# The order of the first loads on SyncE's queue, fixed by hand, in a two-layer decoder on one Trainium2 core

## The chip, the core and the metric

The kernel runs on one core of a Trainium2 chip (trn2). The core has a matrix engine (TensorE, PE in the profile, its weight loads PEld), a vector engine (VectorE, DVE), a scalar engine (ScalarE, ACT), a general engine (GpSimd, POOL) and a synchronisation engine (SyncE, SP) that does nothing here but issue transfers. SP issues its transfers one after the other: a transfer that has to wait holds all those behind it. POOL issues the indirect ones (gathers and scatters). Both kinds are carried by the same 16 DMA engines.

The metric is the device time of one execution in microseconds, as the median of several runs. The kernel before took 3494.49 us (three runs, 3491.88 to 3496.33).

## The reference

Eight sequences of 256 tokens with 512 features go through two layers of three residual steps each. All is float32.

```
x = x + L0_attn(layernorm(x))              # 16 heads, rotary, causal window of 64
x = x + L0_xattn(layernorm(x), ctx, mask)  # cross attention over ctx
x = x + L0_ffn(layernorm(x))               # 64 experts, top 6, capacity 192, and a shared one
x = x + L1_attn(layernorm(x))              # Mamba2 scan, chunks of 64
x = x + L1_xattn(layernorm(x), ctx, ctx)   # attention over features
x = x + L1_ffn(layernorm(x))               # 8 low-rank adapters on one wide network
```

Of `L0_attn` the beginning matters here: `qkv = x @ w_qkv.T`, then the rotary turn of q and k with tables `cos` and `sin`, then masked scores. Of `L0_ffn` it matters that each of the 64 experts has its own `Wg`, `Wu` (512x352 each) and `Wd` (352x512), and computes `(silu(buf @ Wg.T) * (buf @ Wu.T)) @ Wd.T` for its 192 slots.

## The kernel before

The 2048 tokens are 16 tiles `x0` to `x15` of 128 tokens; a batch is two of them. They are loaded once, stay in on-chip memory, each stage adds into them, and the last stage writes them out. The stages follow one another: `l0_attention`, `l0_cross` (which carries the routing and the shared expert in its gaps), `l0_experts`, `l1_mamba` (which begins with gathering the experts' results), `l1_cross`, `l1_ffn`.

**Who sets the order.** The program is written as one sequence. A scheduler then chooses for each engine the order in which its instructions stand, except that instructions given to `pin` (line 95) keep the program's order among themselves. Nearly all matmuls are pinned (`mm`, line 99). Of the transfers on SP some are (the context loads of line 441, the shared expert's of 670 to 684), most are not. Which engine waits for what follows from the tiles that an instruction reads and writes.

**Weights.** All large weights go through one pool of eight buffers of 1 MB (`wpool`, line 74). `weight` (line 88) takes a buffer and issues the load on SP; the load waits until the former user of the buffer is done. Such loads were not pinned.

**The first loads.** `load_constants` (line 102) issues, in this order, the table `c_const` (386 KB), the 16 token tiles (256 KB each), `c_cols`, `c_rows` (1035 KB, one row spread over 128 partitions), `c_small`, and `norm`. Then `l0_attention` (line 182) issues the three projection weights q, k, v (1024 KB each), the output weight `wo`, and the table `const0` with mask, `cos` and `sin` (576 KB). `load_constants` also fills `nhalf`, which `layernorm` reads.

**The start of l0_attention.** For each batch, `normal` normalises the two token tiles on DVE (statistics, then one pass; the root on POOL), `turn` turns them on PE and ACT copies the result to `xnT`, `features` projects 256 features of q or k (called for k0, q0, k1, q1) and turns them by the rotary tables: an ACT copy, a DVE shuffle, two POOL products, a DVE sum. `values` projects v. `step` makes scores and masked maxima. Work of later batches is laid between that of earlier ones (table `between`).

**The expert stage.** `l0_experts` (line 881) handles experts in pairs. Its loads and the products that use them:

```
def load(pair, h):                                     # line 906
    w["g", h] = self.weight(a["Wg"][e]...)             # 704 KB
    w["u", h] = self.weight(a["Wu"][e]...)             # 704 KB
    nc.sync.dma_start(wd[:, 0, :], a["Wd"][e, :P, :])  # 256 KB, line 913
    nc.sync.dma_start(wd[:112, 1:, :], ...)            # 448 KB, line 914
```

`hidden(pair, h, m)` computes one of three blocks of an expert's hidden layer, with eight matmuls on Wg's columns ahead of eight on Wu's (as the trace counts them). `first(pair, h)` multiplies the first 128 slots by Wd, and writes the result to `y_d` on SP (line 939). `last(pair)` does so for the other 64 slots of both experts (two writes, line 954). On PE, a pair p goes in this order:

```
hidden(p,0,0)  first(p-1,1)  last(p-1)  hidden(p,0,1)  hidden(p,0,2)  turn
hidden(p,1,0)  first(p,0)    hidden(p,1,1)  turn  hidden(p,1,2)  turn
```

`turn` transposes gathered tokens `xg` of the next pair, which POOL gathers from `xn_d` (line 893). The writes to `y_d` are not pinned.

Of the kernel before, what the change touches and what calls it, by code (L numbers as in the profile page):

```python
# [7 lines left out]
F32 = mybir.dt.float32  # L8
# [10 lines left out]
P = 128  # L19
B, S, D = 8, 256, 512  # L20
T = B * S
NT = T // P
HC = D // P
# [24 lines left out]
NORM_W = {"sel": 56, "spread": HC * P}  # L48

COL_W = {"bq": 4, "bk": 4, "conv_b": 6, "conv_w": 24, "norm_w": 4, "b1": 16, "end": 1}  # L50

ROW_W = {
    "bv": D, "bo": D, "ln_g": D, "ln_b": D, "br": E1,
    "dt_bias": NH1, "A_log": NH1, "D": NH1, "res": 1, "gamma": 1,
}

SMALL_W = {"gate": HC * E0, "wr": HC * E1, "wdt": HC * NH1}
# [3 lines left out]
def offsets(widths):  # L61
    at, out = 0, {}
    for name, w in widths.items():
        out[name] = (at, at + w)
        at += w
    return out


class Decoder:
# [18 lines left out]
    def weight(self, src, n, w, rows=P):  # L88

        t = self.wpool.tile([P, 2048], F32, tag="w", name="w")  # L90
        v = t[:rows, : n * w].rearrange("p (n w) -> p n w", n=n)
        self.nc.sync.dma_start(v, src)
        return v

    def pin(self, ins):
# [3 lines left out]
    def mm(self, out, lhs, rhs, start=True, stop=True):  # L99
        self.pin(self.nc.tensor.matmul(out, lhs, rhs, start=start, stop=stop))  # L100

    def load_constants(self):
        nc, a = self.nc, self.a
        c = self.cpool.tile([P, sum(CONST_W.values())], F32, name="c_const")
        nc.sync.dma_start(c, a["const"])
        for name, (lo, hi) in offsets(CONST_W).items():
            setattr(self, name, c[:, lo:hi])
        self.x = []
        for i in range(NT):
            t = self.xpool.tile([P, D], F32, name=f"x{i}")  # L110
            nc.sync.dma_start(t, a["x"][i * P : (i + 1) * P, :])
            self.x.append(t)
        c = self.cpool.tile([P, sum(COL_W.values())], F32, name="c_cols")
        nc.sync.dma_start(c, a["cols"])
        self.col = {k: c[:, lo:hi] for k, (lo, hi) in offsets(COL_W).items()}
        c = self.cpool.tile([P, sum(ROW_W.values())], F32, name="c_rows")
        nc.sync.dma_start(c, a["rows"].partition_broadcast(P))
        self.row = {k: c[:, lo:hi] for k, (lo, hi) in offsets(ROW_W).items()}
        c = self.cpool.tile([P, sum(SMALL_W.values())], F32, name="c_small")
        nc.sync.dma_start(c, a["small"])  # L120
        self.small = {k: c[:, lo:hi] for k, (lo, hi) in offsets(SMALL_W).items()}
        self.norm = self.stage_constants(self.cpool, "norm", NORM_W)

        self.in_order = False
        self.nhalf = self.cpool.tile([P, 16], F32, name="c_nhalf")
        nc.vector.memset(self.nhalf, -0.5)

    def stage_constants(self, pool, name, widths):
        c = pool.tile([P, sum(widths.values())], F32, name=name)
        self.nc.sync.dma_start(c, self.a[name])  # L130
        return {k: c[:, lo:hi] for k, (lo, hi) in offsets(widths).items()}

    def rsqrt(self, pool, v, eps, tag):
# [48 lines left out]
    def l0_attention(self):  # L182
# [7 lines left out]
        nc, a = self.nc, self.a  # L190
        LEAD = 10
        W = 3 * P // 2
        wq, wk, wv = (
            self.weight(a["wqkv"][:, i * D : (i + 1) * D].rearrange("(c p) o -> p c o", p=P), HC, D)
            for i in range(3)
        )
        wo = self.weight(a["wout0"].rearrange("(c p) o -> p c o", p=P), HC, D)
        head = lambda j: slice(j * HD, (j + 1) * HD)
        half = lambda h: slice(h * S, (h + 1) * S)
        pairs = [i ^ 1 for i in range(32)]  # L200
        with ExitStack() as ctx:
# [7 lines left out]
            nc.vector.tensor_copy(minus, self.third.unsqueeze(2).to_broadcast([P, HC, P]))  # L209
            at = self.stage_constants(one, "const0", STAGE0_W)  # L210
            mask, keep, cos, sin = (at[k] for k in ("mask", "keep", "cos", "sin"))
            sel, spread = self.norm["sel"], self.norm["spread"]
            made = {b: {} for b in range(B)}

# [175 lines left out]
            for n in range(-16, 8 * B + 18):  # L390
                if n >= -LEAD:
                    step(n)
                for lag, which in ((2, "acc"), (3, "sums")):
                    p = n - lag
# [1116 lines left out]
def decode(tc, a, out):  # L1511
    with ExitStack() as ctx:
        d = Decoder(ctx, tc, a, out)
        d.load_constants()
        with ExitStack() as late:
            d.l0_attention()
            combine = d.l0_moe(late)
            d.l1_mamba(combine)
        d.l1_cross()
        d.l1_ffn()  # L1520
# [96 lines left out]
```

## Time and profile before

| | |
|---|---|
| median of the runs | 3494.49 us |
| the profiled execution, by the clock of the runs | 3501.66 us |
| its span in the profile | 3499.9 us |
| mean granted clock of PE | 0.957 |
| PE busy | 3245.4 us |
| 1185 to 1990 us (experts): PE busy, DMA share, GB/s | 802.4 of 805 us, 0.74, 234 |
| 1990 to 2370 us (mamba): PE busy | 294.7 of 380 us |
| 2370 to 2745 us (l1_cross): PE busy | 359.4 of 375 us |

The profile is that of one execution. "Busy" is time in which an engine had an instruction in work. A row of the timeline gives start and length in us, engine, source line, operation, the tiles written and read, how many like it follow each other, and in brackets how long the engine stood idle before and what ended that. SPq rows are the issue of transfers, not the transfer itself. A row of the windows gives for each stretch the length, the busy time of PE, PEld, DVE, ACT and POOL, and last the granted clock of PE (1.00 is full), the share of the 16 DMA engines' time and GB/s. In the table of transfers the last two numbers are the size of one and the us from issue to landing, where a waiting instruction shows it.

### The profile page before, as it was taken

To read this page: it belongs to the slowest core of one execution; us is meant where nothing else is said; L and a number is where in the kernel's file an instruction comes from. 1 tells how busy PE (TensorE), PEld (TensorE's weight loads), DVE (VectorE), ACT (ScalarE), POOL (GpSimd) and SP (SyncE) were. 2 spreads that over 40 slices of the span, in tenths; PEclk is the share of its full clock that TensorE was granted. 3 is DMA by queue.
4 is the path that set the end of the run, shared out by engine and by line. 5 is a ranking of instruction groups with operands and counts; after the bars stand their busy time and mean duration, and the time that the engine had idled before them with its cause. 6 is when DMAs were issued, how large, how long until landed. Compare 5 with 4: busy or idle time off the path is not lost.

```text
span 3499.9 us, 46993 instructions
## 1 busy us (share of the span) xinstructions
PE 3245.4 (93%) x18803; PEld 2111.6 (60%) x18803; DVE 1551.1 (44%) x3744; ACT 994.2 (28%) x1959; POOL 759.5 (22%) x792
## 2 busy tenths in 40 slices
PE   6999888899989899999999767998999899999999
PEld 4666555555555687877777544663444466666665
DVE  3655588777764100000000178665666333333332
ACT  1222123333332122222222123441555322222221
POOL 2222001222225211111110187332111111111111
PEclk9999989999999999999999869997999899999999
DMA  4000020000000477777777653001000000000000
GB/s 173 1 1 1 7 63 18 11 13 13 26 15 21 135 234 240 236 240 232 240 236 238 224 158 100 1 25 54 28 27 17 34 7 7 5 1 7 6 6 12
DMA packets 106810, 272.56 MB, mean 78 GB/s; under 512 B 15136, under 2 KB 23968, under 8 KB 105696
## 3 DMA queue, kind: packets, MB, share of 16 engines
q1 hardware_dynamic: 88128, 219.16, 19.1%
q0 software_dynamic: 18464, 50.40, 5.2%
q8 instruction: 148, 2.42, 0.3%
q14 instruction: 70, 0.57, 0.1%
HBM read 235.81 MB, written 33.70 MB: 77 GB/s over the span
## 4 chain that ended last, share of the span: by engine, by line
PE 66%; DVE 10%; POOL 6%; issue 3%; DMA 1%; ACT 1%; POOLq 0%; SPq 0%; DVEq 0%; ACTq 0%
PE mm L100 17%; PE sc L100 15%; PE out L100 7%; PE w L100 6%; PE s L100 4%; PE a L100 3%; PE b L100 3%; PE sums L100 2%; PE acc L100 2%; PE st L100 2%; POOL map_d L765 1%; PE pt L903 1%; PE rt L100 1%; DVE acc L1043 1%; POOL ye L648 1%
## 5 line engine op out<-in xcount | busy, mean ns | idle before, releaser
L100 PE MATMUL sc<-xgT,w 128*112 128x192 f32 (+1 forms) x3072 | 529.6, 328 | 0.0
L100 PEld LDWEIGHTS sc<-xgT,w 128*112 128x112 f32 (+1 forms) x3072 | 497.4, 182 | 41.1 <-issue 40.9
L929 DVE TENSOR_TENSOR aT<-act,sc 112x192 f32<-112x192 f32 (+1 forms) x192 | 68.0, 354 | 740.9 <-ACT act L928 740.9
L100 PE MATMUL mm<-xnT,w 128*128 128x256 f32 x1152 | 275.9, 395 | 22.0 <-DMA w<-in_wqkv 15.7
L100 PE MATMUL mm<-w,aT 112*128 112x512 f32 (+3 forms) x768 | 262.7, 596 | 0.0
L100 PEld LDWEIGHTS mm<-xnT,w 128*128 128x128 f32 x1152 | 223.7, 198 | 59.1 <-issue 18.5
L100 PE MATMUL w<-xnT,w 128*128 128x256 f32 x1024 | 243.0, 380 | 0.0
L100 PE MATMUL out<-w,mix 128*128 128x512 f32 x512 | 240.4, 592 | 0.0
L1460 DVE TENSOR_TENSOR h<-base,b 128x512 f32<-128x512 f32 x128 | 88.1, 688 | 327.0 <-PE b L100 327.0
L893 POOL DMA_INDIRECT xg<-xn_d,slots x96 | 90.7, 945 | 641.5 <-PE pt L903 634.1
L100 PEld LDWEIGHTS w<-xnT,w 128*128 128x128 f32 x1024 | 192.3, 191 | 61.2 <-issue 40.4
L1464 POOL TENSOR_TENSOR mix<-h 128x256 f32<-128x256 f32 x128 | 92.8, 725 | 610.8 <-DVE h L1462 547.3
L140 POOL TENSOR_TENSOR lnr<-lne,c_nhalf 128x1 f32<-128x1 f32 x112 | 68.9, 619 | 715.1 <-DVE lne L138 585.4
L1321 DVE TENSOR_REDUCE m<-s 128x1 f32<-128x512 f32 x256 | 164.8, 685 | 102.6 <-PE s L100 84.0
L100 PE MATMUL st<-q,k 32*128 32x256 f32 (+1 forms) x1024 | 196.7, 545 | 9.4 <-ACT e L503 9.3
L1270 ACT ACTIVATE e<-st 128x512 f32<-128x512 f32 x256 | 138.9, 595 | 142.3 <-PE st L100 140.6
L928 ACT ACTIVATE act<-sc 112x192 f32<-112x192 f32 (+1 forms) x192 | 63.4, 330 | 402.2 <-PE sc L100 402.2
L100 PEld LDWEIGHTS out<-w,mix 128*128 128x128 f32 x512 | 97.3, 190 | 122.4 <-issue 120.3
L100 PE MATMUL mm<-mT,w 128*118 128x256 f32 (+1 forms) x768 | 169.7, 379 | 1.1 <-DVE hT L821 1.1
L100 PEld LDWEIGHTS mm<-w,aT 112*128 112x128 f32 (+3 forms) x768 | 95.6, 163 | 122.5 <-issue 122.5
L100 PE MATMUL s<-k,q 32*128 32x512 f32 x512 | 159.5, 697 | 6.7 <-issue 3.5
L100 PEld LDWEIGHTS mm<-mT,w 128*118 128x118 f32 (+1 forms) x768 | 138.9, 181 | 34.3 <-issue 7.2
(333 smaller groups left out, 5287.7 us busy)
## 6 DMA issues: line engine op xcount, KB each, us to landing
w<-in_Wg SPq DMA_DIRECT2D x64, 704.0 KB, 8.1
w<-in_Wu SPq DMA_DIRECT2D x64, 704.0 KB, 4.2
w<-in_Wd SPq DMA_DIRECT2D x64, 448.0 KB, 6.7
w<-in_Wd SPq DMA_DIRECT2D x64, 256.0 KB
y_d<-yo SPq DMA_DIRECT2D x64, 256.0 KB, 4.2
y_d<-yo SPq DMA_DIRECT2D x64, 128.0 KB, 4.1
w<-in_W SPq DMA_DIRECT2D x8, 1024.0 KB, 5.1
x<-in_x SPq DMA_DIRECT2D x16, 256.0 KB, 5.7
```

The costliest lines, as they stand in the source:

```text
L100: self.pin(self.nc.tensor.matmul(out, lhs, rhs, start=start, stop=stop))
L140: ins = nc.gpsimd.tensor_tensor(r, e, self.nhalf[:, :n], ALU.pow)
L648: nc.gpsimd.indirect_dma_start(y, None, y_d, bass.IndirectOffsetOnAxis(ap=read[:, k, i : i + 1], axis=0))
L765: self.pin(nc.gpsimd.indirect_dma_start(maps[k % 2], bass.IndirectOffsetOnAxis(ap=work[b]["write"][:, i, k : k + 1], axis=0), tok[:, 2 * b ...
L893: nc.gpsimd.indirect_dma_start(xg, None, xn_d, bass.IndirectOffsetOnAxis(ap=slots[:, i : i + 1], axis=0))
L903: self.pin(nc.tensor.transpose(t[:, blk], w[n][:, blk], self.ident))
L928: nc.scalar.activation(act[:n_m], ps[:n_m, :CAP], AF.Silu)
L929: nc.vector.tensor_tensor(w["a", h][:n_m, m, :], act[:n_m], ps[:n_m, S : S + CAP], ALU.mult)
L1270: nc.scalar.activation(w["e"][kc][:, j, :], st, AF.Exp, scale=SCALE)
L1321: nc.vector.tensor_reduce(m, sc, AX.X, ALU.max)
L1460: nc.vector.tensor_tensor(both(h), twice(base), both(t), ALU.add)
L1464: nc.gpsimd.tensor_tensor(mix, h[:, :G], h[:, G:], ALU.add)
```

## The change

`weight` and `stage_constants` issue through a new `load`, which pins the transfer. The first loads are split into `load_first` (c_const and the first batch's tokens), `load_tokens` (the tokens of one batch) and `load_last` (c_cols, c_rows, c_small). `l0_attention` loads the weights of k, q and v in this order, then `const0`, then the other tokens, `wo`, `norm` and `load_last`. No arithmetic changes.

```
     def weight(self, src, n, w, rows=P):
...
-        self.nc.sync.dma_start(v, src)
+        self.load(v, src)
...
+    def load(self, dst, src):
+        self.pin(self.nc.sync.dma_start(dst, src))
+
-    def load_constants(self):
+    def load_first(self):
...
         c = self.cpool.tile([P, sum(CONST_W.values())], F32, name="c_const")
-        nc.sync.dma_start(c, a["const"])
+        self.load(c, a["const"])
...
+        self.x = [self.xpool.tile([P, D], F32, name=f"x{i}") for i in range(NT)]
+        self.load_tokens(0)
...
+    def load_tokens(self, b):
+        for i in (2 * b, 2 * b + 1):
+            self.load(self.x[i], self.a["x"][i * P : (i + 1) * P, :])
+
+    def load_last(self):
...
     def stage_constants(self, pool, name, widths):
         c = pool.tile([P, sum(widths.values())], F32, name=name)
-        self.nc.sync.dma_start(c, self.a[name])
+        self.load(c, self.a[name])
...
-        wq, wk, wv = (
+        wk, wq, wv = (
...
-            for i in range(3)
+            for i in (1, 0, 2)
         )
-        wo = self.weight(a["wout0"].rearrange("(c p) o -> p c o", p=P), HC, D)
...
             mask, keep, cos, sin = (at[k] for k in ("mask", "keep", "cos", "sin"))
+            for b in range(1, B):
+                self.load_tokens(b)
+            wo = self.weight(a["wout0"].rearrange("(c p) o -> p c o", p=P), HC, D)
+            self.norm = self.stage_constants(self.cpool, "norm", NORM_W)
+            self.load_last()
...
-        d.load_constants()
+        d.load_first()
```

`weight` is called not only there: `l0_cross` (line 410), `l0_experts` (909, 910), `l1_mamba` (986 to 989) and `l1_ffn` (1346 to 1348) load through it. In the program built from the changed kernel, the order on PE and ACT is the same as before; it differs on SP, and on DVE and POOL among the first instructions.

More of the change, by code (lines that the diff above doesn't have):

```diff
@@ L100, in mm @@
         self.pin(self.nc.tensor.matmul(out, lhs, rhs, start=start, stop=stop))
-    def load_constants(self):
+    def load(self, dst, src):
+        self.pin(self.nc.sync.dma_start(dst, src))
+    def load_first(self):
         nc, a = self.nc, self.a
         c = self.cpool.tile([P, sum(CONST_W.values())], F32, name="c_const")
-        nc.sync.dma_start(c, a["const"])
+        self.load(c, a["const"])
         for name, (lo, hi) in offsets(CONST_W).items():
             setattr(self, name, c[:, lo:hi])
[L108 to L122, printed above, removed]
+        self.x = [self.xpool.tile([P, D], F32, name=f"x{i}") for i in range(NT)]
+        self.load_tokens(0)
         self.in_order = False
@@ L126, in load_constants @@
         nc.vector.memset(self.nhalf, -0.5)
+    def load_tokens(self, b):
+        for i in (2 * b, 2 * b + 1):
+            self.load(self.x[i], self.a["x"][i * P : (i + 1) * P, :])
+    def load_last(self):
+        a = self.a
+        c = self.cpool.tile([P, sum(COL_W.values())], F32, name="c_cols")
+        self.load(c, a["cols"])
+        self.col = {k: c[:, lo:hi] for k, (lo, hi) in offsets(COL_W).items()}
+        c = self.cpool.tile([P, sum(ROW_W.values())], F32, name="c_rows")
+        self.load(c, a["rows"].partition_broadcast(P))
+        self.row = {k: c[:, lo:hi] for k, (lo, hi) in offsets(ROW_W).items()}
+        c = self.cpool.tile([P, sum(SMALL_W.values())], F32, name="c_small")
+        self.load(c, a["small"])
+        self.small = {k: c[:, lo:hi] for k, (lo, hi) in offsets(SMALL_W).items()}
     def stage_constants(self, pool, name, widths):
         c = pool.tile([P, sum(widths.values())], F32, name=name)
-        self.nc.sync.dma_start(c, self.a[name])
+        self.load(c, self.a[name])
         return {k: c[:, lo:hi] for k, (lo, hi) in offsets(widths).items()}
```

## The prediction

> **What bounds the kernel now.** I read the page first, then the timeline of the first 45 us, the waits, and one 25 us period of the expert stage.
>
> ```profile
> span 3499.9 us, 46993 instructions
> PE 3245.4 (93%) x18803; PEld 2111.6 (60%) x18803; DVE 1551.1 (44%) x3744; ACT 994.2 (28%) x1959; POOL 759.5 (22%) x792
> PE 66%; DVE 10%; POOL 6%; issue 3%; DMA 1%; ACT 1%; POOLq 0%; SPq 0%; DVEq 0%; ACTq 0%
> ```
>
> TensorE (PE) is busy for 93% of the span and holds 66% of the chain that ended last. A load costs time only where PE stands still for it. At the start it does:
>
> ```profile
> 11.56 0.59 ACT L233 COPY xnT<-mm 128x512 f32<-128x512 f32 x1 [0.27 <-PE mm L232]
> ...
> 14.42 3.31 SPq L92 DMA_DIRECT2D w<-in_wqkv  x3
> ...
> 27.22 15.85 PE L100 MATMUL mm<-xnT,w 128*128 128x256 f32 x64 [15.69 <-DMA w<-in_wqkv]
> ```
>
> Batch 0's tokens are normalised and turned at 12.15 us. The weights are only issued at 14.42, behind all 16 token tiles and four constant tables, and PE stands for 15.69 us. The expert stage is the opposite: in 1185 to 1990 us PE is busy for 802.4 of 805 us, with DMA at 0.74 of its capacity. There the question is how early a load is issued before its use.
>
> ```profile
> 1367.20 5.46 PE L100 MATMUL sc<-xgT,w 128*112 128x192 f32 x32
> 1367.29 0.33 SPq L92 DMA_DIRECT2D w<-in_Wg  x1
> ...
> 1367.95 1.09 SPq L954 DMA_DIRECT2D y_d<-yo  x2
> ...
> 1369.14 0.56 SPq L92 DMA_DIRECT2D w<-in_Wu  x1
> ...
> 1372.68 0.33 SPq L92 DMA_DIRECT2D w<-in_Wg  x1
> ...
> 1378.92 0.33 SPq L939 DMA_DIRECT2D y_d<-yo  x1
> ...
> 1382.64 0.33 SPq L92 DMA_DIRECT2D w<-in_Wu  x1
> ...
> 1384.18 2.77 PE L100 MATMUL sc<-xgT,w 128*128 128x192 f32 x16
> ```
>
> The Wg and Wu issued at 1367.29 and 1369.14 belong to the pair that starts at 1384.18: about 15 us ahead. The Wg and Wu at 1372.68 and 1382.64 belong to that pair's second expert, which starts 13.7 us into it, at 1397.9: again 15 us or more.
>
> **The change part by part.** There are two parts: the first loads get a new order, and every `weight` load in the kernel becomes pinned. I compared SP's queue in the two built programs.
>
> Start. Ahead of wk there stand only c_const, x0 and x1, 386+512 KB. The new queue is these, wk, wq, wv, const0, then x2 to x15, wo, norm and the rest. With wk that is 1.97 MB. By the DMA rows of 0 to 8.5 us the queue had moved so much by 8.2 us; the old wk landed 2.4 us after its bytes were through by the same count (24.8 against 27.2), so wk lands at about 10.6. On VectorE the statistics of x2 and x3 no longer stand ahead of x0's normalisation: the first turn moves from 9.55 to about 8.6, xnT is done near 11.3, and that, not wk, is last. First projection: 27.2 to 11.5, 15.7 us earlier. Price: the statistics of x2 to x8 (7 x 0.69) and three normalisations (3 x 0.55) fall among the rotations of batch 0, 6.5 us of VectorE work that lay in its idle time before. In the new VectorE order x4's statistics and a normalisation precede q0's shuffle, and two normalisations k1's; counted through, the first masked maximum comes some 2.5 us later against PE than before, and PE's second score block waits for it. wq and wv land about 3 and 6 us after wk and are wanted 5.5 us and 16 us after; const0, near 17, is wanted at 18; x2 and x3 likewise. Net -13 us. norm, wo and the tables move behind 8 MB and land by 30 us, before their first use at about 75: nothing.
>
> Expert stage. The pin moves Wg and Wu past the result writes `y_d`, which are not pinned. Built order around one pair, the kernel before above, the changed one below (g2 = Wg of the next pair's first expert, g3 of its second; y0, y1, yy the writes of `first(p,0)`, `first(p,1)`, `last(p)`):
>
> ```
> before: y1(p-1) g2 yy(p-1) u2 d2 d2 g3 y0(p) u3 d3 d3 y1(p) ...
> after:  y0(p) g2 u2 d2 d2 | y1(p) yy(p) g3 u3 d3 d3 | y0(p+1) ...
> ```
>
> So g2, u2 now wait for the result of `first(p,0)`. In the row, that product ends on PE at F = 1378.1, the write is issued at F+0.8, g2 at F+1.25. PE then has 6.1 us of other work until it wants g2 (1384.18), and 7.4 until it wants u2, the second half of that block. Before the change the loads stood 11 us before F, and the Wu at 1382.64 was hidden by a whole 12 us. When does u2 land now? No row shows this burst. Bytes flow about 1 us after issue and at 340 GB/s (270 to 431 in the rows of 1368 to 1373). The write, g2 and u2 are 262+721+721 KB: 5.0 us from F+1.8. Then a tail from last byte to landing, between two rows:
>
> ```profile
> w<-in_Wg SPq DMA_DIRECT2D x1, 704.0 KB, 4.0
> ```
> ```profile
> w<-in_Wd SPq DMA_DIRECT2D x1, 448.0 KB, 5.6
> ```
>
> The first (issued at 1106.9 into an empty queue) gives 4.0-1.0-2.1 = 0.9 us. The second (1358.96, right behind a Wu of 704 KB and with another Wd after it) lands at 1364.6, while 1180 KB from 1358.7 are through at 1362.2: 2.4. u2 has two Wd behind it, so I take 2.1, near the second: F+8.9, a stall of 1.5 us (0.3 to 1.8). For g3, u3: they now follow `last(p)`, which ends at L = 1367.27 in the row; its two writes are issued by L+1.77 and g3 at L+1.87. PE's other work is 5.66 us, 6.95 until u3. g3's bytes flow from L+2.9; 1442 KB take 4.25; with the tail L+9.25: stall 2.3 (1.1 to 2.6). Sum 3.8 us for each of 31 pairs (the first pair's loads don't wait for a write): **+118 us**.
>
> Two rules of the Trainium skill would make less of this. "DMA: Bandwidth & Descriptors", section on the anatomy of one DMA, fits a transfer as 2.0 us plus bytes / 436e3 (for the GpSimd queue). By it u2 lands at F+0.8+5.9 = F+6.7 and u3 at L+1.87+5.3 = L+7.2: stalls of 0 and 0.2, 6 us in all. The row of 5.6 us is 1180 KB in 6.9 from the first issue where the fit has 4.7, so I go by the rows. "TensorE: Matmul & The Clock Gate", Part 1, lets the clock halve after an idle window of some 3.4 us; stalls of 1.5 and 2.3 us would then cost nothing more. The trace is stricter:
>
> ```profile
> 88.00:90.00 2.00, 1.20 (x23) 0.76 (x20) 1.07 (x8) 1.54 (x3) 0.31 (x1) 1.00 0.00 0
> 90.00:92.00 2.00, 0.98 (x20) 0.77 (x20) 1.92 (x10) 0.72 (x2) 0.00 (x0) 1.00 0.00 0
> 92.00:94.00 2.00, 1.88 (x22) 1.61 (x23) 1.25 (x6) 0.25 (x1) 0.00 (x0) 0.58 0.02 4
> ```
>
> PE idled 1.8 of 4 us (second number) and the granted clock (third from the end) went to half for 3.2 us. Over the span, idle of about 1.5 us in 4 was followed by half clock once in 8 cases, of about 2 in 3 of 6. I take half of the second stalls: 31 x 0.5 x 1.6 us = **+24**, by the rule 0, at most 31 x 2 x 1.6 = 99.
>
> Entry to the experts. In the old queue experts 0 and 1 were mostly loaded before the routing was known; now their 4.3 MB are issued after both `part` reads, from 1173.7. Weights of expert 0 land by about 1180 (wanted at 1188); but the first gather, 6.84 us at 1178.51 behind 1.4 MB, meets more. Against it, the `part` read has no Wu ahead any more and the gathers start about 2 us sooner. +1 (-3 to +4).
>
> Hand-over to mamba. Before, the last result writes (1988.59) lay behind W1 loads and the first combine gather started only at 1996.30. Now W1 and W2 stand at the end of l1_cross, and Wz, Wxbc, wout behind the writes: the gather starts near 1992 but beside 3.6 MB of weights. -2 (-4 to +3). W1 and W2 are issued after 2674 and wanted after 2765; 8.4 MB at 340 GB/s take 25 us: hidden by the rest of l1_cross.
>
> Sum: -13+118+24+1-2 = +128. The profiled execution took 3501.7 us by the clock of the runs, 7.2 above the median of the runs shown, which I take off: 3494.5+128 = **3622 us**.
>
> **Rivals.** *The loads still land in time* (the fit holds): -13+1-2, and 3481 us. For it: DMA's spare quarter. Against: 6 us of slack with a write and 1.4 MB ahead. The point that decides is u2 by F+7.4. Chance 0.07. *Small stalls*, tail 0.9 as in the empty queue: 0.3+1.1 per pair, 43 us and no cold clock: 3522. Chance 0.22. *The burst interleaves*, so that g and u land with the Wd behind them: 2.4 MB in 7.0 us, F+9.7 and L+10 with a tail of 0.9: 2.3+3.1 per pair, 167 us and 50 for the clock: 3698. For it: the packets of the two Wd at 1359 to 1363 were seen mixed. Chance 0.14. *The start gains nothing* (const0 or x2 late, VectorE the next wait) with the stalls as forecast: 3635, inside the first case's range.
>
> **How the numbers follow.** Forecast case 0.57, 3570 to 3665. The range 3510 to 3695 takes in the small stalls and all but the end of the interleaved case. A measurement here tells 0.2%, 7 us, from no change. Faster by more: 0.06, from the first rival; within: 0.03; slower: 0.91.
>
> **What would show it.** First projection at about 11.5 us, not 27.2. In the expert stage 31 pairs with two gaps each on PE, both ended by a Wu or Wg load, a period near 29 us where it is 25, half clock in some slices. If the period stays at 25 us, the stall step is wrong and the change is a gain. If the gaps end with Wd or with `y_d`, the burst is not in order.

## The result and the profile after

The changed kernel takes 3543.35 us (median of four runs, 3541.46 to 3548.98), the kernel before 3494.96 us (3491.88 to 3496.33; the 3494.49 above was the median before its fourth run was there). The ratio is 1.0141, with a 95% interval of 1.0126 to 1.0157: slower by 48.4 us, where 128 were forecast. The direction and the place were right, the size was not.

From the page of the changed kernel: span, busy times, granted clock by slice, shares of the chain that ended last, the costliest group, and two rows of the DMA issues (the last number is the median time to landing).

```profile
span 3540.8 us, 46991 instructions
PE 3265.0 (92%) x18803; PEld 2110.6 (60%) x18803; DVE 1551.4 (44%) x3744; ACT 995.0 (28%) x1959; POOL 757.6 (21%) x792
...
PEclk9999989999999999999999968997999899999999
...
PE 59%; DVE 10%; DMA 9%; POOL 5%; issue 3%; ACT 1%; SPq 0%; POOLq 0%; DVEq 0%; ACTq 0%
...
L100 PE MATMUL sc<-xgT,w 128*112 128x192 f32 (+1 forms) x3072 | 547.4, 331 | 38.7 <-DMA w<-in_Wg 21.7
...
w<-in_Wg SPq DMA_DIRECT2D x64, 704.0 KB, 4.6
w<-in_Wu SPq DMA_DIRECT2D x64, 704.0 KB, 5.7
```

The costliest group on the page of before, for comparison:

```profile
L100 PE MATMUL sc<-xgT,w 128*112 128x192 f32 (+1 forms) x3072 | 529.6, 328 | 0.0
```

DMA was 1% of the chain and is now 9%. The experts' matmuls, which waited for nothing before, now have 38.7 us of idle time ahead of them, most of it put down to Wg. Part of the delay does not show as idle time: the same group is busy for 547.4 us where it was 529.6. The clock row stays at 9 in all slices of the expert stage (14 to 23): none of them shows much half clock.

Both programs run the same 18,803 matmuls in the same order on PE, so their starts can be subtracted one by one. This gives the change by stage. It sums to 40.9 and not 48.4, since the profiled execution of before took 3501.7 us by the clock of the runs, 6.7 above its median, and that of the changed kernel 3542.6:

| stage (us of before) | start of a PE matmul, after minus before | this stage | forecast |
|---|---|---|---|
| start, to 100 | 0 to -13.8 | -13.8 | -13 |
| to the experts, 1200 | -14.0 | -0.2 | +1 |
| experts, 1200 to 1982 | +47.7 | +61.7 | +118 and +24 |
| hand-over, to 2015 | +43.4 | -4.3 | -2 |
| mamba, to 2600 | +41.0 | -2.4 | 0 |
| to the end | +40.9 | -0.1 | 0 |

Start, timelines of PE: the first fence from the changed kernel, the second the same score block in the kernel before.

```profile
11.59 16.76 PE L100 MATMUL mm<-xnT,w 128*128 128x256 f32 x64 [0.68 <-ACT xnT L245]
...
34.63 0.81 PE L233 MATMUL s<-k,q 32*128 32x192 f32 x8 [1.90 <-DVE m L306]
```
```profile
47.37 0.81 PE L221 MATMUL s<-k,q 32*128 32x192 f32 x8
```

The first projection starts 15.6 us earlier and now ends with xnT, not with a load. Then 0.9 is lost inside the projections (16.76 against 15.85 us) and 1.9 at the second score block, which waits for VectorE's maximum; about 1 us is won back between 50 and 60 us. The 0.9 is clock: PE begins the projections at half clock, with a matmul each 0.427 us, and goes on with one each 0.216 us. The first part lasted 5.45 us here and 3.65 us before, and between 2.9 and 6.2 us in the kernels of the experiments.

Expert stage, the timeline of the same pair as in the prediction:

```profile
1366.38 1.09 SPq L966 DMA_DIRECT2D y_d<-yo  x2
1367.56 0.54 SPq L103 DMA_DIRECT2D w<-in_Wg  x1
1368.19 0.40 SPq L103 DMA_DIRECT2D w<-in_Wu  x1
...
1372.33 1.54 PE L100 MATMUL sc<-xgT,w 128*128 128x192 f32 x8 [0.81 <-DMA w<-in_Wg]
...
1374.09 1.57 PE L100 MATMUL sc<-xgT,w 128*128 128x192 f32 x8 [0.22 <-DMA w<-in_Wu]
...
1375.49 2.74 PE L100 MATMUL mm<-w,aT 128*128 128x512 f32 x6
...
1378.88 0.33 SPq L951 DMA_DIRECT2D y_d<-yo  x1
1379.30 0.38 SPq L103 DMA_DIRECT2D w<-in_Wg  x1
1379.77 0.40 SPq L103 DMA_DIRECT2D w<-in_Wu  x1
...
1385.57 0.46 PEld L100 LDWEIGHTS sc<-xgT,w 128*128 128x128 f32 x3 [0.26 <-DMA w<-in_Wu]
```

The queue stands as the prediction said: writes of `last`, then g3 and u3; write of `first`, then g2 and u2. `last(p)` ends at L = 1365.70 (the product of 5.47 us from 1360.23), and g3 is issued at L+1.86 (forecast L+1.87). `first(p,0)` ends at F = 1378.23, and g2 is issued at F+1.07 (F+1.25). PE waits for Wg or Wu before both experts of this pair, as of most. The waits are only smaller than forecast: the bracketed idle times are 0.81 and 0.22 before the second expert, and 0.26 on PE's weight load before the first. By the differences of the matmuls, the second expert's delay has a median of 1.41 us over 30 pairs (forecast 2.3), the first expert's 0.22 (forecast 1.5).

### The profile page after: what moved, and what is told of

Read it like the earlier page. It is cut to its first block, busy times and chain, and to the rows that moved or that the text cites. A ratio compares the mean times of both kernels' runs of the same rounds, so it can differ in the third digit from the quotient of the medians.

```text
span 3540.8 us, 46991 instructions
## 1 busy us (share of the span) xinstructions
PE 3265.0 (92%) x18803; PEld 2110.6 (60%) x18803; DVE 1551.4 (44%) x3744; ACT 995.0 (28%) x1959; POOL 757.6 (21%) x792
## 4 chain that ended last, share of the span: by engine, by line
PE 59%; DVE 10%; DMA 9%; POOL 5%; issue 3%; ACT 1%; SPq 0%; POOLq 0%; DVEq 0%; ACTq 0%
PE mm L100 17%; PE sc L100 9%; DMA w<-in_Wu 7%; PE out L100 7%; PE w L100 6%; PE s L100 4%; PE a L100 3%; PE b L100 3%; PE sums L100 2%; PE acc L100 2%; PE st L100 2%; POOL map_d L777 2%; PE rt L100 1%; DVE acc L1055 1%; DMA ye<-y_d,read 1%
## 5 line engine op out<-in xcount | busy, mean ns | idle before, releaser
L100 PE MATMUL sc<-xgT,w 128*112 128x192 f32 (+1 forms) x3072 | 547.4, 331 | 38.7 <-DMA w<-in_Wg 21.7
```

## The experiments

**The two parts alone.** First only the order of the first loads, with later weights unpinned as before (`ordered` is set to False behind attention 0's loads):

```
     def weight(self, src, n, w, rows=P):
-        self.load(v, src)
+        if self.ordered:
+            self.load(v, src)
+        else:
+            self.nc.sync.dma_start(v, src)
```

> The new order of the first loads stays, but weight loads after attention 0 are not pinned. If the time was lost to the pin on the experts' Wg and Wu alone, the first projection starts at 11.6 us, the expert stage has the 24.98 us period of before again, and the time is 3495-13.8 = 3481 us. If the stalls have something to do with the start's new order (VectorE's and SP's order there shifts what follows), it stays above 3500.

Measured: 3485.16 us, ratio 0.9968 (0.9956 to 0.9980), 11.4 us faster than the kernel before in the same set of runs (3496.51 us; from the experiment without the Wd loads on it is 3498.33 us). The row of the expert stage, one window of this kernel (sum, then busy PE, PEld, DVE, ACT, POOL, granted clock, DMA share, GB/s):

```profile
1167.00:1972.00 805.00, 801.18 (x4224) 634.50 (x4224) 67.99 (x192) 177.19 (x385) 86.82 (x92) 1.00 0.74 235
```

PE is busy for 801 of 805 us again, and the differences of the matmuls show 0.00 us in every pair. So the start's order has no part in the stalls. Then the pin alone, in the kernel before:

```
     def weight(self, src, n, w, rows=P):
-        self.nc.sync.dma_start(v, src)
+        self.pin(self.nc.sync.dma_start(v, src))
```

> The kernel before with one edit: the load in weight is pinned. No order of the first loads. By the trace of the changed kernel (in its expert stage the distance to the kernel before grew by 60 us, in the hand-over it shrank by 5) this gives 3495+60-5 = 3550 us, with the same two gaps per pair (0.2 and 1.4 us). If the two parts help or hurt each other (the earlier start moves the loads against each other), it differs by more than 5 us from that; my forecast's own term for this part was +118 and +24 for the clock, 3635 us.

Measured: 3557.34 us (3550.40 to 3571.14), ratio 1.0181 (1.0161 to 1.0200), 60.8 us slower. That is 7 more than expected, with runs that scatter over 20 us; medians of the delay are 1.32 us for the second expert and 0.41 for the first. The parts add up within the scatter: -11.4+60.8 = 49.4, and both together gave 48.4.

**All pins but those of Wg and Wu.** This keeps the pinned order at the hand-over.

```
-            w["g", h] = self.weight(a["Wg"][e]...., HC, M0)
-            w["u", h] = self.weight(a["Wu"][e]...., HC, M0)
+            w["g", h] = self.weight(a["Wg"][e]...., HC, M0, pin=False)
+            w["u", h] = self.weight(a["Wu"][e]...., HC, M0, pin=False)
```

> The changed kernel with the pin taken off Wg and Wu alone: first loads in order, and the weights of attention 1, mamba and the feed-forward pinned. If the 5 us between 1950 and 2400 us are a gain of the pinned order at the hand-over (result writes before Wz, W1 and W2), the time is 3495-13.8-5 = 3476 us. If they were only given back stalls (the combine had been waiting for something else), it is 3481.

Measured: 3480.04 us, ratio 0.9949 (0.9935 to 0.9962): faster than both kernels, by 16.5 us than before. Between the experts' last matmul and mamba's first its PE gains 4.7 us on before; the kernel with the first loads alone gains none there (it loses 0.5). The seven other traces with the later loads pinned gain 4.2 to 4.9 there. So the hand-over's gain belongs to the pinned order. It is seen in the wait ahead of mamba's first transposes, in the timeline of before and then of the changed kernel:

```profile
2015.35 1.11 PE L1017 MATMUL pt<-c_const,xn 128*128 128x128 f32 x4 [27.44 <-DVE xn L154]
```
```profile
2058.80 1.12 PE L1029 MATMUL pt<-c_const,xn 128*128 128x128 f32 x4 [23.20 <-DVE xn L162]
```

**The pin kept, the loads called one expert earlier.**

```
+        load(0, 0)
         for pair in range(E0 // 2):
             for h in range(2):
-                load(pair, h)
                 for m in range(3):
...
                     if m == 0:
+                        e = 2 * pair + h + 1
+                        if e < E0:
+                            load(e // 2, e % 2)
                         for work in late:
```

> The changed kernel with all its pins, but each expert's loads are called one expert earlier in the program, so that they stand one expert (12.5 us) earlier in SP's queue, still behind a result write. If lateness of the loads is the whole of the loss, no gap of over 0.3 us on PE ends with Wg or Wu, and the time is that of the kernel with unpinned experts, 3476 to 3481 us. The Wu of a pair's second expert then waits on SP for the buffer that last() of the pair before releases, 7 us ahead of its use. If that wait blocks the queue too long, or if a pinned load costs time by itself, it stays above 3495.

Measured: 3482.91 us, ratio 0.9963 (0.9949 to 0.9977). SP's timeline in one pair of this kernel:

```profile
1365.96 0.33 SPq L951 DMA_DIRECT2D y_d<-yo  x1
1366.38 0.38 SPq L103 DMA_DIRECT2D w<-in_Wg  x1
1369.68 0.33 SPq L103 DMA_DIRECT2D w<-in_Wu  x1
1370.98 0.33 SPq L925 DMA_DIRECT2D w<-in_Wd  x1
```

The Wg still stands right behind a result write, and the Wu waits for its buffer (3 us after Wg). Yet no wait of PE ends with Wg or Wu in the stage, and no pair is delayed. Here Wg and Wu are issued 14 to 19 us before PE uses them (before: 16 to 25; in the changed kernel 4.7 to 5.8, medians). So the pin by itself costs nothing in this stage; the late issue does.

**What stands behind the burst.** The forecast gave u2 and u3 a tail of 2.1 us between last byte and landing, because two Wd loads follow them. In this kernel all experts but the first use the first one's Wd, so that nothing follows Wu:

```
+            if e == 0:
+                t = pool.tile([P, 2048], F32, tag="wd0", name="wd0", bufs=1)
...
-            nc.sync.dma_start(wd[:, 0, :], a["Wd"][e, :P, :])
-            nc.sync.dma_start(wd[:112, 1:, :], ...)
+            wd = w["d", h] = self.wd0
```

> The changed kernel without the Wd loads of experts 1 to 63 (all experts use the first one's Wd, so 704 KB less behind each Wg and Wu). My forecast let u land 2.1 us after its last byte because two Wd follow it, and 0.9 us with nothing behind: by that the stalls shrink by 1.2 us each, to 0.2 and 0, and the time is about 3490. In the changed kernel's packets the 5632-byte ones of Wg and Wu end before the 2048-byte ones of Wd begin; if SP's queue serves transfers in order and what stands behind costs nothing, the stalls stay at 1.4 and 0.2 us and the time at 3543 (within 10).

Measured: 3536.89 us, ratio 1.0111 (1.0095 to 1.0126). Delays of 1.22 us before the second expert and 0.16 before the first (medians), 49 us over 30 pairs where the changed kernel has 60. It is 38.6 us slower than the kernel before, the changed kernel 48.4. What follows thus costs 0.2 us (medians) to 0.4 us (sums) a pair for both stalls together, not the 1.2 us a stall on which the forecast rested.

**The order inside the burst**, Wu ahead of Wg:

```
-            w["g", h] = self.weight(a["Wg"]...)
             w["u", h] = self.weight(a["Wu"]...)
+            w["g", h] = self.weight(a["Wg"]...)
```

> The changed kernel with Wu loaded ahead of Wg; PE still wants Wg first. If the loads land one after the other in order of issue, Wg now lands where Wu did (7.4 us after first(), 8.3 us after last() ends) and is wanted at 6.1 and 5.9: stalls of 1.3 and 2.4 us instead of 0.2 and 1.4, 2.1 us a pair or 65 us more, 3608 us. Stalls of 2.4 us should now bring the half clock as the one of 2.2 us at 1721 us did: 1.4 us each, and then 3651. If the clock doesn't follow, 3608. If both land together, the order makes no difference and it stays at 3543.

Measured: 3676.62 us, ratio 1.0509 (1.0495 to 1.0523), 25 us beyond the higher figure. Two lines of PE's timeline, second expert and then first:

```profile
1399.28 2.84 PE L100 MATMUL sc<-xgT,w 128*128 128x192 f32 x16 [3.09 <-DMA w<-in_Wg]
...
1412.37 2.84 PE L100 MATMUL sc<-xgT,w 128*128 128x192 f32 x16 [1.60 <-DMA w<-in_Wg]
```

Now each block has one wait, for the load that stands second. The loads land one after the other, and half clock is back: 30 spells (stretches at half clock) in the expert stage, where the changed kernel has one. PE waits 128.9 us for Wg in the stage; the loss against before is 197 us. The spells last 112.6 us together, so half clock can explain at most 56 us of the remaining 68.

**Wd ahead of both**, its two loads pinned as well:

```
+            t = self.wpool.tile([P, 2048], F32, tag="w", name="w")
...
             w["g", h] = self.weight(a["Wg"]...)
             w["u", h] = self.weight(a["Wu"]...)
```

> The changed kernel with both Wd loads ahead of Wg and Wu. In order of issue 721 KB more at 430 KB/us are 1.7 us: Wu lands 9.1 us after first() and 10.0 after last(), wanted at 7.4 and 7.0, stalls of 1.7 and 3.0, 4.7 us a pair against 1.6: 95 us more, 3638. With half clock after each second stall (31 x 1.4) 3681; with half clock after both 3724. If Wd's packets interleave with the others wherever they stand, it stays near 3543.

Measured: 3790.03 us, ratio 1.0833 (1.0814 to 1.0852), beyond all three figures, with 38 spells of half clock in the stage. PE's timeline shows why:

```profile
1410.58 6.98 PE L100 MATMUL mm<-w,aT 128*128 128x512 f32 x18
...
1427.88 2.58 PE L100 MATMUL sc<-xgT,w 128*128 128x192 f32 x7 [4.50 <-DMA w<-in_Wg]
```

The row of 6.98 us is the product that takes 5.47 at full clock. `last` ends at 1417.56 and Wg is there only at L+10.3. In the packets of this burst Wd's 721 KB took from 1420.5 to 1423.4, 2.9 us where 1.7 were put: its packets of 2048 bytes moved 250 KB/us, those of 5632 bytes behind them some 400 in the middle of their stretch. Order of issue decides, as expected; the price of what stands ahead was too low.

**Tokens of batches 2 to 7 last**, in the kernel with unpinned experts:

```
-            for b in range(1, B):
-                self.load_tokens(b)
+            self.load_tokens(1)
...
             self.load_last()
+            for b in range(2, B):
+                self.load_tokens(b)
```

> The kernel with unpinned experts (3480 us) and one more edit: the tokens of batches 2 to 7 stand last among the first loads, so that VectorE's order has fewer of their statistics and normalisations among batch 0's rotations (two of x2's and x3's and none of x4's before q0's shuffle). If the 2.5 us that the start gained less than the first projection (27.2 to 11.6 is 15.6; 13 to 13.8 are left) are those instructions, the time is about 2 us less, 3478. If the next wait is PE's own or the tables', nothing changes: 3480.

Measured: 3486.27 us, ratio 0.9965 (0.9952 to 0.9979): no gain, rather 3 us of the start lost in its trace. All statistics of x4 to x8 but one did leave the rotations of batch 0, but from the first projection to the first masked maximum it still takes 22.0 us, as in the changed kernel (21.9; before 18.6). VectorE's timelines show where. The four shuffles of batch 0 (k0, q0, k1, q1) start this far apart:

| | k0 to q0 | q0 to k1 | k1 to q1 |
|---|---|---|---|
| before | 3.94 | 3.95 | 3.94 |
| changed | 5.29 | 5.02 | 3.95 |
| tokens 2 to 7 last | 5.90 | 3.96 | 4.54 |

That is 2.4 us more than before in the changed kernel and 2.6 here, where both normalisations of x2 and x3 stand ahead of q0's shuffle. The other 0.9 and 0.8 us are the longer half clock in the first projections. That clock also makes 1.2 of the 3 us lost here: the projections took 16.66 us, 15.49 in the kernel with unpinned experts.

## Why the prediction was wrong in size

**Start**: right, -13 forecast and -13.8 found. The projection is 15.6 us earlier (15.7), VectorE's first masked maximum comes 2.4 us later against PE (2.5), and PE's second score block waits for it, as named. That the sum fits within 0.8 us is in part luck: the 0.9 us of longer half clock were not in it, and about 1 us came back later. The reason given for the price holds only in part: taking away the statistics of x4 to x8 did not lower it. What is left among the rotations is the work for x2 and x3, and that was not tried alone.

**Expert stalls**: the mechanism was right, its size not. The step that failed is "u2 has two Wd behind it, so I take 2.1": the tail from last byte to landing. The packets of Wg and Wu are the only ones of 5632 bytes, so their ends can be read from the trace:

| | last packet of Wu, forecast | found | PE has Wu, forecast | found |
|---|---|---|---|---|
| u2, after `first` | F+6.8 | F+6.86 (1385.09) | F+8.9 | F+7.34 (1385.57) |
| u3, after `last` | L+7.15 | L+7.85 (1373.55) | L+9.25 | L+8.38 (1374.08) |

The tail is 0.5 us both times. Over 62 experts the time from Wu's last packet to PE's use of Wu has a median of 0.49 us at the first expert of a pair and 0.48 at the second. The bytes were the smaller error, of the other sign: the 1442 KB of Wg and Wu took 4.7 us (median; some 307 KB/us where 340 were put), and u3's came 0.7 us later than forecast. With 0.5 in its own sum, and u3's bytes as found, stall 1 is 0 and stall 2 is 1.4 us, which are the medians found (0.22 and 1.41).

The 2.1 came from a row that I misread. These are the loads on SP of the kernel before at that place:

```profile
1357.66 0.33 SPq L92 DMA_DIRECT2D w<-in_Wu  x1
1358.96 0.33 SPq L913 DMA_DIRECT2D w<-in_Wd  x1
1359.34 0.48 SPq L914 DMA_DIRECT2D w<-in_Wd  x1
```

The 448 KB with 5.6 us to landing are those of line 914, issued at 1359.34, not at 1358.96. So the other Wd stood ahead of this load and not behind it, 1442 KB had to flow and not 1180, and it landed at 1364.94. The last packet of the two Wd ended at 1364.05: the tail was 0.9 us, not 2.4. Both rows would then have given 0.9, and the sum stalls of 0.3 and 1.1 us, which I had given to a rival. Even the 0.9 of the load into the empty queue was partly flow: its last packet ended 0.36 us before it landed. The kernel without the Wd loads shows that followers hardly count. Over 30 pairs the delays sum to 49.9 us before the second expert and 10.0 before the first; medians alone would give 49 together, and a few pairs with 2 to 4.5 us make the rest.

The fit from the Trainium skill's page "DMA: Bandwidth & Descriptors" (its section on the anatomy of one DMA), which was weighed against the rows, was off on the other side: it put u3 at L+7.2, found is L+8.4, forecast 9.25. For stall 1 it was nearer than the forecast: F+6.7 against F+7.34 and 8.9. It is a fit of single transfers, and here two or three stood in line. The row that was held against it, read rightly, is 1442 KB in 7.3 us from the first issue, where the fit has 5.3.

**Half clock**: +24 forecast, one spell found, worth at most 1.7 us (half of its 3.41). The reading behind it was not wrong: it asked what idle of 2.3 us would do (though the spell that it gives 3.2 us, at 92 us, has 3.41). With Wu ahead of Wg there are 33 gaps on PE of 2.0 us or more in the stage, and 30 were followed by half clock; of 28 gaps from 1.0 to 2.0 us, none. Most of the changed kernel's gaps lie below that, so the term fell with the stall it was hung on. But length alone does not decide. With Wd first only 38 of 59 gaps of 2.0 us or more were followed, and one of 3.44 us was not. The changed kernel's one spell follows a wait of 2.22 us (at 1721.11), while its longest, 2.30 us (at 1316.67), was not followed. The last section says what decides. These are windows of the changed kernel:

```profile
1720.29:1723.71 3.42, 1.20 (x9) 0.97 (x8) 0.35 (x1) 0.92 (x2) 0.95 (x1) 1.00 0.89 310
1723.71:1727.12 3.41, 3.04 (x11) 2.54 (x10) 0.00 (x0) 0.00 (x0) 0.00 (x0) 0.50 0.80 216
1185.00:2030.00 845.00, 806.35 (x4138) 621.44 (x4137) 66.66 (x188) 171.28 (x374) 81.87 (x87) 1.00 0.67 216
```

In the first, PE (second number) stands still for 2.22 of 3.42 us; in the next, the clock (third number from the end) is 0.50; over the whole stage it rounds to 1.00.

**Entry and hand-over**: -0.2 for +1, and -4.3 for -2. Whether the two effects named at the entry cancelled as described is not shown. That W1 and W2 come late and hidden was right: nothing changes after 2600 us. The -2.4 inside mamba was not foreseen, and it isn't settled: other kernels with the same hand-over show between +0.4 and -5.5 there.

**Rivals.** "Small stalls" with the tail of 0.9, 43 us and no cold clock, came nearest: 3522 forecast (its own terms give 3523.5), 3543 found. It too had the tail too long and u3's bytes too early; what it had nothing for are the pairs with 2 us and more. "The loads still land in time" and "the burst interleaves" are out: PE waits in every pair but the first, and Wd's packets hardly start before Wu's have ended. So is "the start gains nothing".

## What to carry to other kernels

A helper that pins one kind of transfer changes its place against all the unpinned ones: look at every caller, and ask of each load how far ahead of its use it is now issued. Keep pins where the order is wanted (the first loads, the hand-over) and either leave a double-buffered stream to run ahead or call its loads one step earlier; these gave 11 to 17 us here where the pin as made lost 48. When a stall is the small difference of two times of 7 to 9 us, an error of 1.6 us in one of them is the whole forecast: make sure which transfer a row is (its line, its size, its issue, what stands ahead of it), and take the tail from a load of the same kind.

## What the runs showed of the hardware

**The clock goes by steps.** In each of the ten traces here all changes of the granted clock lie whole multiples of 3.413 us apart (within 0.003 us). I cut the expert stage of the five kernels with late loads into these steps, 1285 of them at full clock. In the 70 that were followed by half clock, PE stood still for 2.00 us or more of the step; in the 1215 others for 1.95 us or less. So a wait counts only with the part that falls into one step. The kernel with the pin alone also has a wait of 2.22 us, from 1630.08 on, and no half clock:

```profile
1628.25:1631.67 3.42, 1.54 (x8) 1.27 (x8) 0.08 (x1) 0.39 (x1) 0.94 (x1) 1.00 1.00 309
1631.67:1635.08 3.41, 2.78 (x12) 2.06 (x13) 0.35 (x1) 0.33 (x1) 0.00 (x0) 1.00 0.49 121
```

PE stands still for 1.88 us of the first step and for 0.63 of the second. An estimate from this: a wait of 2.3 us at a random place is followed by half clock in (3.41 - 2.3 + 2 x 0.3) / 3.41, half of all cases, which is what the forecast took. Outside the expert stage each trace has a few steps with less idle time (down to 0.05 us) that were followed by half clock too; these are not explained.

In the three kernels with late loads and Wg first (the changed one, the pin alone, the one without Wd) there are 91 gaps of 0.5 to 2.0 us in the expert stage, and half clock followed none. Of the four longer ones it followed two.

**A coincidence.** The largest delays of the changed kernel, 4.5 us (at 1723) and 3.3 us (at 1319), fall where one packet of 16 KB of the instruction queue had started 3 to 4 us before PE wanted Wg, and kept one of the 16 DMA engines for 0.9 and 1.6 us. At 1723 all but 40 KB of Wg and Wu were through by 1724.5, and the rest took up to another 0.9 us. Three pairs with 2.6 to 2.9 us have no such packet near, so this is a coincidence in two cases and not shown as a cause.
